# Statistics loads on another queue, and the last group's spectra packed into one block diagonal

## The chip, the cores and the metric

The kernel runs on one core of a Trainium2 chip: a tensor engine (PE), a vector engine (DVE), a scalar engine (ACT), GpSimd (POOL) and a sync engine (SP) that here only issues transfers. Transfers are also issued by ACT and GpSimd. The metric is the time of one execution on the device in microseconds, of which less is better.

## The reference

The input x holds 32 images of 32 channels of 128 x 128. Two layers are computed, each on a group-normalised x and added to it (eps 1e-5, 16 groups of two channels):

```python
# layer 1: five steps of a coupled iteration for a matrix square root, per image and channel
Y = A / norm(A); Z = I
for _ in range(5):
    T = 0.5 * (3.0 * I - Z @ Y)
    Y = Y @ T
    Z = T @ Z
x = x + Y * sqrt(norm(A))                     # A = groupnorm(x)
# layer 2: a spectral convolution
f = real(fft2(groupnorm(x)))                  # 32 low and 32 high rows, 32 columns are kept
top = einsum('bixy,ioxy->boxy', f[:, :, :32, :32], weights1)
bot = einsum('bixy,ioxy->boxy', f[:, :, -32:, :32], weights2)
x = x + real(ifft2(top and bot in their places, zeros elsewhere))
```

The second layer needs the first layer's whole image for its statistics, and its weights mix the 32 input channels at each of the 2048 kept frequencies.

## The kernel before, in words

**Iteration.** A unit of work is four channels of one image. `fetch` loads x and its transpose (tiles `b` and `xt`, 256 KB each, on ACT's queue), `staged` normalises them, and `newton` runs the iteration as a Python generator of some 13 steps: four matmuls of 128 x 128 into one PSUM bank, then an eviction by DVE (`plus`, L242) or ACT (`taken`, L234 and L236). Four lanes run such generators side by side; the main loop (L775) takes one step of each per round, so that the PE always has another lane's products to do.

**Statistics of an image.** `prep` (L160) loads the transposed image in eight tiles `xs` of 256 KB, three buffers, on SP's queue, takes `bn_stats` of each on DVE (L175), then goes through a short chain of moments, roots and reciprocals on DVE, ACT and PE, and leaves in `made` the scales that `staged` reads. One step of it is taken per round, at lane 1. Three loads are issued ahead; then each step takes the statistics of one tile and issues the load three tiles on. `stage` starts the preparation of an image when the image before it begins.

**After the iteration.** `settle` stores a finished tile to the DRAM tensor `mid` (L335, SP's queue) and folds it for the transform; `forward` and `spectrum` transform, take the second layer's statistics, and store the spectrum to the DRAM tensor `xs` of the image's group (L449). The 32 images form three groups, `GROUPS = (21, 8, 3)`.

**Products with the weights.** When a group's last spectrum is stored, `follow` starts its products. The first group goes through `wide_products`: the weights stand in a block diagonal. Groups of at most `NB = 8` images go through `small_products` (L512): the spectra stand in a block diagonal and the weights are the moving operand. A place for spectra is a tile of 128 x 2048, four diagonal blocks of 32 rows by 8 images by 64 numbers; what is off the diagonal is cleared once. There are two such tiles (`diags`) and, in the tail, three more (`late_xks`), cleared by DVE (L783). For a step `kk` of 16, 32 matmuls of 32 x 32 blocks fill a quarter of each of four column strips of PSUM; after every second step ACT copies the bank to a tile `om` (L569), which SP stores to the DRAM tensor `od` in one transfer of 256 KB (L534). SP's loads of spectra (L526) are four per pair of steps, one for each diagonal block.

**Inverse.** `inverse` loads a group's products (L590) and the tiles of `mid` (`yt`, 512 KB, L605), transforms back, adds, and stores to `out` (L613). It starts when the products of its group are all issued. Tiles `yt` alternate between six buffers and, in the tail, four more from the pool `late`. Tiles `om`, the reloaded products of a small group, and the differences `d` share three buffers tagged `page`.

**The tail.** Once no iteration is left, the pool `sets` of the iteration is closed (L779), its memory becomes the pool `late`, GpSimd loads the weights of the 14 later steps into it (L786, 512 KB each), and stores of the output go to ACT's queue.

**What sets the order.** The program is written with a tile framework which places each engine's instructions by a planner's estimate of when they are ready, and adds the waits. `kept` (`tc.keep_in_program_order`) pins an instruction behind everything written before it for its engine; nearly all transfers are pinned. Each engine, and each engine's queue of transfers, works strictly in order: a transfer that waits for its data or its buffer holds what comes after it on the issuing engine.

Of the kernel before, what the change touches and what calls it, by code (L numbers as in the profile page):

```python
# [24 lines left out]
F32 = mybir.dt.float32  # L25
# [34 lines left out]
def conv_preact_kernel(  # L60
# [32 lines left out]
    xs, od = [], []  # L93
    for i, n in enumerate(GROUPS):
        few = n <= NB
        shape = [KK // 2, P, NB, 64] if few else [KK, P, B, 32]
        xs.append(dram.tile(shape, F32, name=f"xs{i}", tag=f"xs{i}"))
        shape = [KK, 4, 4, NB, 8 * C] if few else [KK, 4, B, L * C]
        od.append(dram.tile(shape, F32, name=f"od{i}", tag=f"od{i}"))
    where = [(i, b) for i, n in enumerate(GROUPS) for b in range(n)]  # L100

# [58 lines left out]
    def prep(b, made):  # L160

        st = small.tile([P, C, 6], F32, tag="a_st", name=f"a_st{b}", bufs=2)
        tiles = []

        def load(i):
            t = stp.tile([P, 4, P], F32, tag="xs", name=f"xs{b}_{i}")
            kept(nc.sync.dma_start(out=t, in_=xt_in[b, :, 4 * i : 4 * i + 4, :]))
            tiles.append(t)

        for i in range(3):  # L170
            load(i)
        yield
        for i in range(C // 4):
            for c in range(4):
                nc.vector.bn_stats(st[:, 4 * i + c, :], tiles[i][:, c, :])  # L175
            if i + 3 < C // 4:
                load(i + 3)
            yield
        _, nm, d = yield from moments(st, "a")
        q = small.tile([P, C], F32, tag="a_qs", name=f"a_qs{b}")  # L180
        nc.vector.tensor_reduce(
            q, d.rearrange("p g (c e) -> p (g c) e", e=2), AX.X, ALU.add
        )
        yield
        pq = bank()[:, 0, 0:C]
        nc.tensor.matmul(pq, avg_mean, q, start=True, stop=True)

        v = small.tile([P, C + G], F32, tag="a_v", name=f"a_v{b}")
        nc.vector.tensor_scalar_mul(v[:, 0:C], pq, -512 / (P * P))
        yield  # L190
        vg = small.tile([P, G], F32, tag="a_vg", name=f"a_vg{b}")
        nc.vector.tensor_reduce(
            vg, v[:, 0:C].rearrange("p (g c) -> p g c", c=2), AX.X, ALU.add
        )
        nc.vector.tensor_scalar(v[:, C:], vg, 0.5, EPS, ALU.mult, ALU.add)
        s = root(v, C + G, "a_r")
        inv = small.tile([P, C + G], F32, tag="a_inv", name=f"a_inv{b}")
        nc.vector.reciprocal(inv, s)
        yield

        sc = small.tile([P, C], F32, tag="a_sc", name=f"a_sc{b}", bufs=2)
        nc.vector.tensor_scalar_mul(sc, inv[:, 0:C], 1.0 / P)
        n = small.tile([P, G, 2], F32, tag="a_n", name=f"a_n{b}")
        nc.vector.tensor_tensor(  # L204
            n,
            s[:, 0:C].rearrange("p (g c) -> p g c", c=2),
            inv[:, C:, None].to_broadcast([P, G, 2]),
            ALU.mult,
        )
        nn = small.tile([P, C], F32, tag="a_nn", name=f"a_nn{b}")  # L210
        nc.vector.tensor_scalar_mul(
            nn, n.rearrange("p g c -> p (g c)"), P * (1.5 / EYE) ** 2
        )
        sn = root(nn, C, "a_t")

        scr = small.tile([P, C], F32, tag="a_scr", name=f"a_scr{b}", bufs=2)
        nc.vector.tensor_scalar_mul(scr, sc, QR * QS)
        off = small.tile([P, G, 2], F32, tag="a_off", name=f"a_off{b}", bufs=2)
        nc.vector.tensor_tensor(
            off,  # L220
            scr.rearrange("p (g c) -> p g c", c=2),
            nm[:, :, None].to_broadcast([P, G, 2]),
            ALU.mult,
        )
        made[b] = (nm, sc, sn, scr, off.rearrange("p g c -> p (g c)"))
        yield
# [285 lines left out]
    def small_products(i):  # L512

        n = GROUPS[i]
        xks = [t.rearrange("p (b m) -> p b m", b=4 * NB) for t in diags] + late_xks
        wts = [t.rearrange("p (e q t o) -> p e q t o", e=2, q=4, t=4) for t in plain] + late_wts

        def load_weights(kk):
            if kk < 2 or not late:
                kept(nc.sync.dma_start(out=wts[kk % len(wts)], in_=wk[kk]))  # L520

        def load_spectra(k2):
            for l4 in range(4):
                rows = slice(32 * l4, 32 * l4 + 32)
                kept(
                    nc.sync.dma_start(  # L526
                        out=xks[k2 % len(xks)][rows, NB * l4 : NB * l4 + n, :],
                        in_=xs[i][k2, rows, 0:n, :],
                    )
                )  # L530

        def store(k2, om):
            kept(
                nc.sync.dma_start(  # L534
                    out=od[i][2 * k2 : 2 * k2 + 2].rearrange("e q l b x -> (q l b) e x"),
                    in_=om.rearrange("p (e x) -> p e x", e=2),
                )
            )

        if i == small_groups[0]:  # L540
            for t in diags:
                nc.gpsimd.memset(t, 0.0)
        for kk in range(2):
            load_weights(kk)
        for k2 in range(len(xks)):
            load_spectra(k2)
        done = None
        for kk in range(KK):
            yield
            k2, e = divmod(kk, 2)  # L550
            wt, xk = wts[kk % len(wts)], xks[k2 % len(xks)]
            if not e:
                pm = bank()
            for t in range(8):
                for q in range(4):
                    nc.tensor.matmul(  # L556
                        pm[32 * q : 32 * q + 32, 2 * e + t // 4, 32 * (t % 4) : 32 * (t % 4) + 32],
                        xk[:, :, 32 * e + 8 * q + t],
                        wt[:, t // 4, q, t % 4, :],
                        start=True,  # L560
                        stop=True,
                    )
            if kk + len(wts) < KK:
                load_weights(kk + len(wts))
            if done and not e:
                store(*done)
            if e:
                om = page(f"om{i}_{k2}")[:, 0:512]
                nc.scalar.copy(om, pm.rearrange("p a x -> p (a x)"))  # L569
                done = k2, om  # L570
                if k2 + len(xks) < KK // 2:
                    load_spectra(k2 + len(xks))
        store(*done)
        yield

# [3 lines left out]
    def load_products(b):  # L579
        if b < B and b not in obs:  # L580
            g, n = where[b]
            few = GROUPS[g] <= NB

            ob = page(f"or{b}") if few else inv.tile([P, 1024], F32, tag="ob", name=f"ob{b}", bufs=2)
            if few:
                src, dst = od[g][:, :, :, n, :].rearrange("k q l x -> (k q) l x"), "p (l x) -> p l x"
            else:
                src, dst = od[g][:, :, n, :].rearrange("k q x -> (k q) x"), "p (l x) -> p (l x)"
            for e in range(2):
                kept(nc.sync.dma_start(out=ob[64 * e : 64 * e + 64].rearrange(dst, l=4), in_=src))  # L590
            obs[b] = ob

    def load_input(b, e):

        if b >= B or (b, e) in yts:
            return
        yts[b, e] = []
        for i in range(2):
            o = 16 * e + 8 * i
            turn = len(yts) + i  # L600
            if late and turn % 2:
                y = late[0].tile([P, 8, P], F32, tag="yt_late", name=f"yt{b}_{o}", bufs=4)
            else:
                y = inv.tile([P, 8, P], F32, tag="yt", name=f"yt{b}_{o}", bufs=6)
            kept(nc.sync.dma_start(out=y, in_=mid[b][:, o : o + 8, :]))  # L605
            yts[b, e].append(y)
# [106 lines left out]


    late = []
    late_xks, late_wts = [], []
    small_groups = [i for i, n in enumerate(GROUPS) if n <= NB]
    lanes = [None] * LANES
    todo = [(b, g) for b in range(B) for g in range(C // 4)]
    fetches = list(todo)  # L720
# [54 lines left out]
    while todo or any(lanes) or posts or specs or prods or backs:  # L775
        tail = not todo and not any(lanes)
        if tail and not posts and not late:

            phase.close()  # L779
            late.append(ctx.enter_context(tc.tile_pool(name="late", bufs=1)))  # L780
            for i in range(3):
                late_xks.append(late[0].tile([P, 4 * NB, 64], F32, name=f"xk{i}_late"))
                nc.vector.memset(late_xks[-1], 0.0)  # L783
            for kk in range(2, KK):
                late_wts.append(late[0].tile([P, 2, 4, 4, C], F32, name=f"wt{kk}_late"))
                nc.gpsimd.dma_start(out=late_wts[-1], in_=wk[kk])  # L786
# [87 lines left out]
```

## Time and profile before

| | |
|---|---|
| time, median of three runs | 3241.55 us (3238.5 to 3243.46) |
| span of the profiled run | 3243.4 us, mean granted PE clock 0.978 |
| PE busy | 3076.9 us, 95% |
| DVE busy | 2302.2 us, 71% |
| GpSimd busy | 1761.7 us, 54% |
| ACT busy | 1462.2 us, 45% |
| transfers | 479.37 MB, mean 148 GB/s |
| statistics loads, issue to landing | 256 of 256 KB, median 3.8 us |
| loads of b, of xt, issue to landing | 256 each of 256 KB, median 2.9 and 3.2 us |

A share over the whole span hides that the program has phases. The row of PE in the page's forty slices stands at 9 (90% or more) from the second slice to the last but two, with one 8 and a few weaker stretches between; DMA traffic is about 100 GB/s in the first 24 slices and 200 GB/s after them, when the inverse transforms of the first group have begun; and the last two slices, with PE at 5 and 4, hold the tail. A wait on an engine costs time only if the PE, or in the tail the chain of transfers, comes to wait for it. So the phases are read one by one.

### The profile page before, as it was taken

To read this page: it belongs to the slowest core of one execution; us is meant where nothing else is said; L and a number is where in the kernel's file an instruction comes from. 1 tells how busy PE (TensorE), PEld (TensorE's weight loads), DVE (VectorE), ACT (ScalarE), POOL (GpSimd) and SP (SyncE) were. 2 spreads that over 40 slices of the span, in tenths; PEclk is the share of its full clock that TensorE was granted. 3 is DMA by queue.
4 is the path that set the end of the run, shared out by engine and by line. 5 is a ranking of instruction groups with operands and counts; after the bars stand their busy time and mean duration, and the time that the engine had idled before them with its cause. 6 is when DMAs were issued, how large, how long until landed. Compare 5 with 4: busy or idle time off the path is not lost.

```text
span 3243.4 us, 78214 instructions
## 1 busy us (share of the span) xinstructions
PE 3076.9 (95%) x30656; PEld 2945.4 (91%) x30656; DVE 2302.2 (71%) x6395; ACT 1462.2 (45%) x3068; POOL 1761.7 (54%) x2310
## 2 busy tenths in 40 slices
PE   6999999999999999999999999999999998999954
PEld 6999999999999999999999999998989888999853
DVE  6777777777777777777777776577777777766654
ACT  3444444444444444444444444444444444445532
POOL 4554555455455544455455454366667776746642
PEclk9999999999999999999999999999999999999985
DMA  3233333332233333333322236665666766576677
GB/s 124 97 103 102 99 105 99 101 98 94 83 100 105 102 99 105 99 102 98 101 93 90 95 100 203 212 214 198 223 224 202 248 231 223 191 221 210 200 253 266
DMA packets 271746, 479.37 MB, mean 148 GB/s; under 512 B 80656, under 2 KB 91408, under 8 KB 271376
## 3 DMA queue, kind: packets, MB, share of 16 engines
q1 hardware_dynamic: 192752, 322.28, 30.6%
q10 hardware_dynamic: 76608, 144.74, 13.9%
q0 software_dynamic: 2016, 7.34, 0.6%
q8 instruction: 242, 3.96, 0.5%
q14 instruction: 128, 1.05, 0.1%
HBM read 319.06 MB, written 155.19 MB: 146 GB/s over the span
## 4 chain that ended last, share of the span: by engine, by line
PE 79%; DMA 8%; DVE 8%; issue 2%; ACT 2%; SPq 1%; POOL 0%; DVEq 0%; ACTq 0%; POOLq 0%
PE ps L248 61%; PE ps L254 10%; DMA xs<-in_xt 6%; DVE xt L326 1%; PE ps L671 1%; PE ps L358 1%; DVE a_st L175 1%; DVE yt L688 1%; PE ps L395 1%; PE ps L556 1%; PE ps L492 1%; DMA or<-od 1%; DVE v L242 1%; PE ps L649 1%; ACT spec L437 1%
## 5 line engine op out<-in xcount | busy, mean ns | idle before, releaser
L340 POOL TENSOR_TENSOR fold<-xt 128x256 f32<-128x256 f32 x512 | 362.6, 729 | 627.2 <-DVE xt L326 566.3
L291 POOL TENSOR_TENSOR r<-b,eye 128x512 f32<-128x512 f32 x256 | 327.1, 1278 | 625.0 <-issue 604.2
L248 PE MATMUL ps<-w,v 128*128 128x128 f32 x4096 | 549.1, 277 | 2.9 <-DVE w L242 2.9
L248 PE MATMUL ps<-y,q 128*128 128x128 f32 x4096 | 545.7, 276 | 0.9 <-ACT y L234 0.9
L248 PEld LDWEIGHTS ps<-w,v 128*128 128x128 f32 x4096 | 501.5, 193 | 5.5 <-DVE w L242 4.0
L248 PEld LDWEIGHTS ps<-y,q 128*128 128x128 f32 x4096 | 501.5, 193 | 2.1 <-ACT y L234 1.3
L234 ACT COPY y<-ps 128x512 f32<-128x512 f32 x512 | 299.5, 585 | 355.9 <-PE ps L248 355.4
L272 POOL TENSOR_SCALAR x<-xt,a_nm,a_sc 128x128 f32<-128x128 f32 x1024 | 448.1, 451 | 20.8 <-DVE a_n L204 19.1
L282 ACT ACTIVATE b<-b,a_off,a_scr 128x128 f32<-128x128 f32 x1024 | 422.7, 486 | 2.1 <-DMA b<-in_x 1.8
L242 DVE SCALAR_TENSOR_TENSOR w<-ps,r 128x512 f32<-128x512 f32 x512 | 348.5, 683 | 60.0 <-PE ps L254 57.9
L242 DVE SCALAR_TENSOR_TENSOR q<-ps,eye 128x512 f32<-128x512 f32 x512 | 348.4, 682 | 59.0 <-PE ps L248 50.9
L624 POOL TENSOR_TENSOR yt<-yt,d 128x512 f32<-128x512 f32 x236 | 300.2, 1298 | 165.0 <-ACT d L683 142.8
L242 DVE SCALAR_TENSOR_TENSOR v<-ps,m 128x512 f32<-128x512 f32 x256 | 175.6, 686 | 256.9 <-PE ps L248 255.1
L315 POOL TENSOR_TENSOR r<-mb,eye 128x512 f32<-128x512 f32 x256 | 326.1, 1274 | 25.3 <-ACT mb L236 25.0
L254 PE MATMUL ps<-ident,v 128*128 128x128 f32 x2048 | 313.2, 276 | 17.1 <-DVE v L242 16.9
L236 ACT ACTIVATE mb<-ps 128x512 f32<-128x512 f32 x256 | 153.1, 598 | 387.2 <-PE ps L254 376.8
L175 DVE BATCH_NORM_STATS2 a_st<-xs 128x6 f32<-128x128 f32 x1024 | 224.0, 279 | 144.9 <-DMA xs<-in_xt 144.0
L326 DVE SCALAR_TENSOR_TENSOR xt<-ps,a_t_s,xt 128x128 f32<-128x128 f32 x1024 | 289.4, 341 | 49.7 <-PE ps L248 49.2
L248 PE MATMUL ps<-m,q 128*128 128x128 f32 x2048 | 284.6, 282 | 22.8 <-DVE q L242 21.3
L242 DVE SCALAR_TENSOR_TENSOR v<-ps,x 128x512 f32<-128x512 f32 x256 | 175.6, 686 | 181.0 <-PE ps L248 180.6
L248 PE MATMUL ps<-y,t 128*128 128x128 f32 x2048 | 281.2, 281 | 9.0 <-DVE t L242 5.4
L248 PEld LDWEIGHTS ps<-m,q 128*128 128x128 f32 x2048 | 251.2, 193 | 36.3 <-DVE q L242 22.6
(119 smaller groups left out, 5252.6 us busy)
## 6 DMA issues: line engine op xcount, KB each, us to landing
b<-in_x ACTq DMA_DIRECT2D x256, 256.0 KB, 2.9
xt<-in_xt ACTq DMA_DIRECT2D x256, 256.0 KB, 3.2
xs<-in_xt SPq DMA_DIRECT2D x256, 256.0 KB, 3.8
mid<-xt SPq DMA_DIRECT2D x256, 256.0 KB, 2.0
yt<-mid SPq DMA_DIRECT2D x128, 512.0 KB, 6.6
out<-yt SPq DMA_DIRECT2D x108, 512.0 KB, 4.6
ob<-od SPq DMA_DIRECT2D x42, 256.0 KB, 4.2
out<-yt ACTq DMA_DIRECT2D x20, 512.0 KB, 5.0
```

Source lines behind the costliest of these rows:

```text
L175: nc.vector.bn_stats(st[:, 4 * i + c, :], tiles[i][:, c, :])
L234: nc.scalar.copy(t, ps)
L242: nc.vector.scalar_tensor_tensor(s, ps, f, t, ALU.mult, ALU.add)
L248: nc.tensor.matmul(ps[:, j, :], lhsT[:, j, :], rhs[:, j, :], start=True, stop=True)
L254: nc.tensor.transpose(ps[:, j, :], t[:, j, :], ident)
L272: nc.gpsimd.tensor_scalar(m[:, j, :], xt[:, j, :], nm[:, c // 2 : c // 2 + 1], sc[:, c : c + 1], ALU.add, ALU.mult,)
L282: nc.scalar.activation(mb[:, j, :], mb[:, j, :], AF.Identity, bias=off[:, c : c + 1], scale=scr[:, c : c + 1],)
L291: nc.gpsimd.tensor_tensor(r, mb, eye, ALU.add)
L315: nc.gpsimd.tensor_tensor(r, mb, eye, ALU.add)
L326: nc.vector.scalar_tensor_tensor(xt[:, j, :], ps[:, j, :], sn[:, c : c + 1], xt[:, j, :], ALU.mult, ALU.add)
L340: nc.gpsimd.tensor_tensor(f[:, :, 64 * half : 64 * half + 64], xt[:, :, 0:64], xt[:, :, 64:128], op)
L624: engine.tensor_tensor(yh, yh, d, op)
```

## The change

It has four parts.

1. The loads of `prep` go to ACT's queue, and the load three tiles on is issued one step later: after the `yield`, ahead of the next tile's statistics. This takes them out of the queue in which stores wait for finished tiles, and lets the statistics that free a buffer end before ACT comes to the load.
2. In `small_products` a group of n < 8 images uses a block diagonal of n images, not of eight. A group of three then needs 768 columns for a place and not 2048, so that two places fit into each of the two `diags` tiles, and the three late tiles and their clearing on DVE go. The two tiles are cleared again by GpSimd for each group, since the blocks lie elsewhere. The matmuls have 4 n stationary columns; their results are 4 n rows in each quarter of the partitions, which are evicted quarter by quarter, by ACT and DVE in turn, and stored in four transfers.
3. The DRAM tensors `xs` and `od` of such a group are laid out to match: `xs` without unused images, `od` with the image innermost among 32 rows of a quarter, so that the 4 n rows of a quarter are adjacent. For the group of eight nothing changes in the layout, the places or the copies.
4. The memory gained goes to the late `yt` tiles: eight buffers and not four.

```diff
@@ prep
-            kept(nc.sync.dma_start(out=t, in_=xt_in[b, :, 4 * i : 4 * i + 4, :]))
+            kept(nc.scalar.dma_start(out=t, in_=xt_in[b, :, 4 * i : 4 * i + 4, :]))
...
                 nc.vector.bn_stats(st[:, 4 * i + c, :], tiles[i][:, c, :])
+            yield
             if i + 3 < C // 4:
                 load(i + 3)
-            yield
@@ small_products
-        xks = [t.rearrange("p (b m) -> p b m", b=4 * NB) for t in diags] + late_xks
+        parts = [slice(32 * q, 32 * q + 4 * n) for q in range(4)] if n < NB else [slice(0, P)]
+        size = 4 * n * 64
+        xks = [
+            t[:, size * j : size * j + size].rearrange("p (b m) -> p b m", m=64)
+            for t in diags
+            for j in range(2048 // size)
+        ]
...
-                        out=xks[k2 % len(xks)][rows, NB * l4 : NB * l4 + n, :],
+                        out=xks[k2 % len(xks)][rows, n * l4 : n * l4 + n, :],
...
-            kept(
-                nc.sync.dma_start(
-                    out=od[i][2 * k2 : 2 * k2 + 2].rearrange("e q l b x -> (q l b) e x"),
-                    in_=om.rearrange("p (e x) -> p e x", e=2),
+            for rows in parts:
+                kept(
+                    nc.sync.dma_start(
+                        out=od[i][2 * k2 : 2 * k2 + 2].rearrange("e q b x -> (q b) e x")[rows],
+                        in_=om.rearrange("p (e x) -> p e x", e=2)[rows],
+                    )
                 )
...
-        if i == small_groups[0]:
-            for t in diags:
-                nc.gpsimd.memset(t, 0.0)
+        for t in diags:
+            nc.gpsimd.memset(t, 0.0)
...
-                        pm[32 * q : 32 * q + 32, 2 * e + t // 4, 32 * (t % 4) : 32 * (t % 4) + 32],
+                        pm[32 * q : 32 * q + 4 * n, 2 * e + t // 4, 32 * (t % 4) : 32 * (t % 4) + 32],
...
-                nc.scalar.copy(om, pm.rearrange("p a x -> p (a x)"))
+                for j, rows in enumerate(parts):
+                    copy = nc.vector.tensor_copy if j % 2 else nc.scalar.copy
+                    copy(om[rows], pm.rearrange("p a x -> p (a x)")[rows])
@@ load_products, load_input
-                src, dst = od[g][:, :, :, n, :].rearrange("k q l x -> (k q) l x"), "p (l x) -> p l x"
+                src, dst = od[g][:, :, n : 4 * GROUPS[g] : GROUPS[g], :].rearrange("k q l x -> (k q) l x"), "p (l x) -> p l x"
...
-                y = late[0].tile([P, 8, P], F32, tag="yt_late", name=f"yt{b}_{o}", bufs=4)
+                y = late[0].tile([P, 8, P], F32, tag="yt_late", name=f"yt{b}_{o}", bufs=8)
@@ main loop, where the iteration has ended
-            for i in range(3):
-                late_xks.append(late[0].tile([P, 4 * NB, 64], F32, name=f"xk{i}_late"))
-                nc.vector.memset(late_xks[-1], 0.0)
```

More of the change, by code (lines that the diff above doesn't have):

```diff
@@ L95, in conv_preact_kernel @@
         few = n <= NB
-        shape = [KK // 2, P, NB, 64] if few else [KK, P, B, 32]
+        shape = [KK // 2, P, n, 64] if few else [KK, P, B, 32]
         xs.append(dram.tile(shape, F32, name=f"xs{i}", tag=f"xs{i}"))
-        shape = [KK, 4, 4, NB, 8 * C] if few else [KK, 4, B, L * C]
+        shape = [KK, 4, 32, 8 * C] if few else [KK, 4, B, L * C]
         od.append(dram.tile(shape, F32, name=f"od{i}", tag=f"od{i}"))
@@ L532, in store @@
         def store(k2, om):
-            kept(
-                nc.sync.dma_start(
-                    out=od[i][2 * k2 : 2 * k2 + 2].rearrange("e q l b x -> (q l b) e x"),
-                    in_=om.rearrange("p (e x) -> p e x", e=2),
-                )
-            )
-        if i == small_groups[0]:
-            for t in diags:
-                nc.gpsimd.memset(t, 0.0)
+            for rows in parts:
[4 more added lines that the diff above has]
+                    )
+                )
+        for t in diags:
+            nc.gpsimd.memset(t, 0.0)
         for kk in range(2):
@@ L715, in conv_preact_kernel @@
     late = []
-    late_xks, late_wts = [], []
-    small_groups = [i for i, n in enumerate(GROUPS) if n <= NB]
+    late_wts = []
     lanes = [None] * LANES
```

## The prediction, made before the changed kernel was run

> **What bounds the kernel now.** I read the page's busy shares first (TensorE 95% busy), then the same shares in stretches of 100 us, then the waits of the stretches that are not full, then the timeline around the longest of them. The stretches (columns: length; busy us and count of TensorE, its weight loads, VectorE, ScalarE, GpSimd; granted TensorE clock; DMA share; GB/s):
>
> ```profile
> core 0: us, PE busy (x) PEld busy (x) DVE busy (x) ACT busy (x) POOL busy (x), PEclk, DMA share, GB/s
> 300.00:400.00 100.00, 99.87 (x899) 96.87 (x898) 72.74 (x213) 45.41 (x94) 51.32 (x73) 1.00 0.30 96
> ...
> 2200.00:2300.00 100.00, 92.86 (x893) 88.70 (x892) 74.27 (x187) 46.18 (x105) 67.50 (x79) 0.97 0.56 190
> ...
> 2600.00:2700.00 100.00, 89.97 (x864) 84.01 (x862) 76.25 (x196) 44.51 (x100) 69.61 (x79) 0.97 0.70 235
> ...
> 3100.00:3200.00 100.00, 46.80 (x1348) 41.57 (x1347) 39.35 (x82) 22.93 (x50) 35.67 (x37) 0.69 0.70 243
> ```
>
> Three phases. From 100 to 2000 us TensorE is idle for 9.7 us in all: nothing taken off another engine can show there. From 2100 to 2900, where the first group's inverse transforms run beside the iteration and DMA traffic doubles, it is idle for 42.2 us (100 less each stretch's busy time, summed), and five of the eight stretches show a granted clock of 0.95 to 0.98, together 15 us of lost clock. From 3124 on no iteration is left, and the last group's products and inverses stand alone.
>
> What ends the idle time in 2100 to 2900, and what the DMA queue of SyncE waits for over the run (total us, times, longest):
>
> ```profile
> DVE a_st L175 <- DMA xs<-in_xt: 50.7, 24, 7.1
> ...
> SPq L335 <- DVE xt L326: 1410.9, 197, 24.5
> ```
>
> VectorE waits 24 times for a statistics load (xs). That load shares SyncE's queue with the stores of finished tiles (L335), which wait for the end of an iteration. The longest case in the timeline (start, length, engine, and in brackets the idle time before):
>
> ```profile
> 2625.49 1.57 SPq L605 DMA_DIRECT2D yt<-mid  x2
> 2627.10 8.17 SPq L167 DMA_DIRECT2D xs<-in_xt  x4
> 2634.04 0.87 DVE L175 BATCH_NORM_STATS2 a_st<-xs 128x6 f32<-128x128 f32 x4 [7.14 <-DMA xs<-in_xt]
> 2634.83 0.67 DVE L242 SCALAR_TENSOR_TENSOR v<-ps,x 128x512 f32<-128x512 f32 x1
> 2635.56 1.11 PE L254 MATMUL ps<-ident,v 128*128 128x128 f32 x4 [5.38 <-DVE v L242]
> ```
>
> The first loads of an image go out only at 2627.10, right behind two 512 KB loads; VectorE had come to its statistics before that and stands for 7.14 us. The v behind them on VectorE is late, and TensorE starves for 5.38 us. I set all TensorE pauses over 0.7 us between 2100 and 2900 beside the xs waits: nine end within 4 us after one (4.25, 1.89, 0.93, 0.87, 2.94, 3.24, 5.38, 1.36, 3.42), 24.3 us in all. The five long ones (4.25, 2.94, 3.24, 5.38, 3.42) lie in exactly the five stretches with the lower clock. So I put 24.3 + 15 = 39 us down to late statistics loads.
>
> The tail:
>
> ```profile
> 3130.13 1.76 DVE L783 MEMSET xk_late<- 128x2048 f32 x1 [0.38 <-issue]
> 3131.82 0.10 DVE L149 COPY b_nm<-ps 128x16 f32<-128x16 f32 x1
> 3132.30 1.76 DVE L783 MEMSET xk_late<- 128x2048 f32 x1 [0.38 <-issue]
> ...
> 3140.95 0.37 SPq L449 DMA_DIRECT2D xs<-spec  x1
> ...
> 3153.12 3.57 SPq L526 DMA_DIRECT2D diag<-xs  x8
> 3156.42 2.09 PE L556 MATMUL ps<-plain,diag 128*32 128x32 f32 x128 [17.38 <-DMA diag<-xs]
> ...
> 3195.17 1.18 SPq L590 DMA_DIRECT2D or<-od  x2
> ...
> 3210.22 15.24 SPq L605 DMA_DIRECT2D yt<-mid  x6
> ```
>
> Clearing the late spectra tiles sits on VectorE between the steps of the last image's moments. The chain goes on through the store of its spectrum, the reload, the products (3156 to 3192), the store and reload of products, and the last three inverses, whose loads of mid stand 15 us waiting for buffers.
>
> **What the Trainium skill says.** "DMA: Bandwidth & Descriptors", section Queues, rings and completion order: the queues of SyncE and ScalarE are one row of rings each, a DMA engine takes descriptors in ring order and goes round robin between rows. So a load in ScalarE's row is not behind the 512 KB loads in SyncE's. The trace agrees: in 2100 to 2900 the median landing is 3.7 us for b (ScalarE's queue) and 5.2 us for transfers that touch xs (59 of 91 are these loads), while in 100 to 2000 it is 2.9 and 3.3. The section Issuing engines are not separate DMA queues says that another issuing engine only saves issue time; the example above shows that here it also changes what a load waits behind. "TensorE: Matmul & The Clock Gate", section What's actually happening: after an idle window of about 3.4 us the clock drops to half, and comes back after about as long at work. That fits the five stretches; 15 us over five pauses is 3 us each.
>
> **The change, part by part.** *Loads to ScalarE's queue.* 256 issues leave SyncE (410 ns median each) for ScalarE, which issues b and xt in 334 and 445 ns. In 100 to 2000 that is 8 per image of some 93 us: 3 us on an engine that is busy 45%, and TensorE has ScalarE's results queued; nothing. In 2100 to 2900, 59 loads. What is queued behind such a load on ScalarE are the copies of y, m, t that TensorE waits for, so a waiting issue would hurt. The load waits for the statistics that free its buffer; putting it one step later (after the yield) lets those finish first, at the price of a lead of two steps and not three: an image takes some 105 us here for 26 rounds, 4 us a step, so 8 us against a landing of 3.7 us median, 8.6 at most. The first three loads still have one step, 4 us. At 2624 to 2626 ScalarE was not behind (d, t, y follow each other), so in the example the load would have gone out about 2.5 us sooner and landed 3.7 later, near 2628.5, leaving a wait of under 2 us, not 7. Between nothing (the one-step lead is too short) and all 39 us, I take half: -19.5. Against it stands ScalarE's standing at issues: four waits there ended by DMA (3.2, 2.3, 2.2, 2.1, together 9.8 us) for 116 issues; 59 more give 5 us, half of it felt: +2.5 (bounds 0 and, if each of 59 held ScalarE for 0.4 us and all of it showed, 24).
>
> *Start.* Image 0's loads now come behind b and xt in one ring (up to +1.5), while image 1's loads, placed behind ScalarE's first activations, no longer bring statistics between the steps of image 0's moments from 18 to 26 us (up to -3). I take -1.
>
> *Clears.* Three memsets of 1.76 us leave VectorE; the chain that ended last holds 0.88 + 1.76 + 1.76 = 4.4 us of them: -4.4. The clear of the two diagonal tiles for the last group comes to GpSimd, 2 x 1.80 us; GpSimd is idle from 3144.5 to 3167.9 and the spectrum lands at 3153 (or 3149): hidden by that transfer, 0. That transfer takes 12.2 us beside the late weights, however early it goes out, so the 4.4 us carry on.
>
> *Small products of the last group.* The same 1024 matmuls with 12 columns and not 32 stationary: TensorE's pace there (2.2 us for 128, then pauses of 1.2 to 4.6 us without a cause in the profile) stays. Four places in place of five: in the old order the last spectra load was issued at 3176.6 and needed at 3188; 16 loads, then 4 loads and 4 stores by turns at 0.42 us put the last at about 25 us after the first, product seven at 35: hidden. Stores: 32 and not 8, 24 x 0.42 = 10 us more issue on SyncE, spread over 36 us in which it waited for evictions; only the last round shows: 3 more issues (1.2) and a second half-microsecond copy per engine (0.6), less a shorter transfer (98 KB and not 256): +1.5. VectorE's copies have nothing behind them.
>
> *Eight late buffers.* The six loads at 3210 need not wait 15 us. But from 3200 to 3236 the DMA engines are 0.91 to 1.04 busy: 12 loads and 12 stores of 0.524 MB, 12.6 MB at about 0.33 MB/us, are 38 us however they are ordered. What is left are gaps: -2 (0 to -5).
>
> The group of eight keeps its layouts, places and copies: 0. Sum: -19.5 + 2.5 - 1 - 4.4 + 1.5 - 2 = -22.9, from 3241.5: 3218.6, rounded 3218.
>
> **Rivals.** (1) *The transfer is late anyway*: one step of lead is too short on ScalarE's ring too, the waits stay, only start and tail gain: 3241.5 - 1 - 4.9 = 3236. For it: the first tiles of an image have the longest waits. Against: in the example the issue itself was late. (2) *ScalarE becomes the place of the wait*: in-order behind loads that wait for VectorE's statistics or an earlier transfer, the copies that feed TensorE come late. 24 us in 2100 to 2900 and 0.2% of the first 2000 (4 us), no gain but the tail's: 3241.5 + 28 - 6 = 3263; half of it, 3250, is as likely. For it: one ScalarE wait of 3.2 us was ended by a transfer. Against: b and xt, 512 issues, cost it so little. (3) *All late loads cured*, SyncE's queue moving freely too: -39 + 2.5 - 5.9: 3199.
>
> **How the numbers follow.** Forecast 0.58, (1) 0.17, (2) 0.16, (3) 0.09. Range 3197 to 3246: from (3) through (1) and the edge of (2). Over 0.2% faster means under 3235: the forecast, (3) and a third of (1), 0.72. Within: 0.12. Slower (over 3248): 0.16.
>
> **What would show it.** Right: waits for xs in 2100 to 2900 at 25 us or less, granted clock at 0.99 or more in most of those stretches, TensorE idle there near 25 us; no memset on VectorE after 3100 and some 4 us less to the last spectrum; the last six loads issued without a pause but the end no more than a few us nearer. Wrong: ScalarE idle before y, m, t by a transfer for over 10 us, or TensorE below 99% in 100 to 2000, speak for (2); xs waits as long as before for (1). A new order of instructions along the whole program, since every one of them is placed anew, could also move some us either way in the middle phase, which none of these steps holds.

## The result, and the profile after

The kernel after takes 3229.99 us (median of 4 runs, 3225.19 to 3232.89) against 3241.64 before: ratio 0.9964 [0.9946, 0.9981], 11.7 us less. The forecast was 3218, so the sign and the range hold, and the size is half of what was forecast. The profiled executions differ by 15.5 us (3243.4 and 3227.9). They can be cut at marks that every kernel has: the issue of the stores of spectra (the transfer xs<-spec, one per image: the 1st, 21st, 31st and 32nd) and the first product of the last group. Each stretch was measured in one profiled execution per kernel. Kernels with the same code up to the end of a stretch agree there within about 3 us; in the last stretch, kernels with the same tail differ by up to 5 us.

| stretch, us | before | after | difference | forecast |
|---|---|---|---|---|
| start to 1st spectrum | 176.9 | 174.6 | -2.3 | -1 |
| 1st to 21st (nothing beside the iteration) | 1779.9 | 1764.0 | -15.9 | 0 |
| 21st to 31st (first group's inverses beside it) | 1119.3 | 1124.7 | +5.4 | -17 |
| 31st to 32nd | 64.8 | 60.6 | -4.2 | -4.4 |
| 32nd to first product | 15.5 | 18.4 | +2.9 | 0 |
| first product to the end | 87.0 | 85.6 | -1.4 | -0.5 |

The gain is not where it was forecast. Where 17 us were to come, the kernel became slower; where nothing was to come, it gained 16 us. These two errors partly cancel, so that sign and range hold by luck. Three stretches of 100 us in the kernel after (columns as before):

```profile
core 0: us, PE busy (x) PEld busy (x) DVE busy (x) ACT busy (x) POOL busy (x), PEclk, DMA share, GB/s
300.00:400.00 100.00, 99.96 (x907) 97.55 (x906) 75.51 (x221) 45.67 (x95) 51.79 (x74) 1.00 0.30 96
2200.00:2300.00 100.00, 94.64 (x918) 89.64 (x917) 75.71 (x198) 47.46 (x105) 67.60 (x80) 0.99 0.63 209
2600.00:2700.00 100.00, 90.71 (x874) 85.16 (x873) 73.79 (x188) 45.20 (x102) 70.38 (x79) 0.97 0.71 232
```

In the first line the busy share hardly moves (99.87 to 99.96), but the count of matmuls goes from 899 to 907: 0.9% more work in the same 100 us. Over 1600 us of this phase, first before, then after:

```profile
300.00:1900.00 1600.00, 1592.34 (x14350) 1542.78 (x14349) 1173.84 (x3435) 731.41 (x1512) 815.51 (x1152) 1.00 0.31 99
```

```profile
300.00:1900.00 1600.00, 1599.28 (x14478) 1555.87 (x14477) 1190.98 (x3469) 737.21 (x1525) 824.28 (x1162) 1.00 0.31 99
```

TensorE's busy time grows by 6.9 us, its matmuls by 128, which at 1600 us for 14478 are 14.1 us of work. So about half of what TensorE lost before stood in the profile as idle time; the other half lay inside what it calls busy. The busy time of its weight loads grows by 13.1 us, and the stretch from the 1st to the 21st spectrum gets 0.9% shorter, as the count says.

In this phase VectorE waited 68.8 us in 44 waits for statistics loads before, and 0.6 us in one wait after. The longest of these waits comes once in each image. In the kernel before:

```profile
354.97 0.37 SPq L449 DMA_DIRECT2D xs<-spec  x1
...
356.01 0.32 SPq L335 DMA_DIRECT2D mid<-xt  x1
...
356.38 1.98 SPq L167 DMA_DIRECT2D xs<-in_xt  x3
...
360.76 0.29 DVE L175 BATCH_NORM_STATS2 a_st<-xs 128x6 f32<-128x128 f32 x1 [2.81 <-DMA xs<-in_xt]
```

SyncE's queue stands 10.0 us before the store of a spectrum (354.97), until its data is there, and 0.6 us before the store of a tile (356.01). An image's first three statistics loads go out right behind them, and VectorE stands 2.81 us before the first. All 18 images from 300 to 1900 us show this order, with waits of 2.3 to 4.3 us.

What ends VectorE's waits for statistics in 2100 to 2900, and SyncE's largest wait over the whole run:

```profile
DVE a_st L175 <- DMA xs<-in_xt: 39.5, 14, 5.6
```

```profile
SPq L335 <- DVE xt L326: 1658.8, 198, 15.1
```

Before, these were 50.7 us in 24 waits and 1410.9. The loads no longer stand behind the finished tiles in SyncE's queue, which waits longer now and holds none of them. But in this phase 14 waits remain of 24, and they are longer in the mean (2.8 us for 2.1). TensorE is idle for 41.5 us of these 800 us (42.2 before), and seven of the eight stretches show a granted clock below 1.00, together 19 us of lost clock (15 before). One of the waits that are left:

```profile
2864.55 0.65 ACTq L262 DMA_DIRECT2D xt<-in_xt  x1
...
2865.30 1.16 ACTq L167 DMA_DIRECT2D xs<-in_xt  x1
...
2872.87 0.49 DVE L175 BATCH_NORM_STATS2 a_st<-xs 128x6 f32<-128x128 f32 x2 [5.62 <-DMA xs<-in_xt]
...
2875.03 1.38 PE L248 MATMUL ps<-m,q 128*128 128x128 f32 x8 [4.13 <-DVE q L242]
```

The load goes out at 2865.30, right behind b (2864.18) and xt, together 512 KB, of ScalarE's own row, and lands 7.6 us later. "DMA: Bandwidth & Descriptors" in the Trainium skill, section Queues, rings and completion order, says that a DMA engine takes one row's descriptors in ring order; this trace agrees: b lands at 2867.88, xt at 2869.12, xs at 2872.85. So the move put the load behind ScalarE's own loads. That is half of the 7.6 us only: a load of 512 KB that SyncE issued at 2866.00 lands at 2872.68, and how much of the second half is due to such traffic was not separated.

A cost that was small before, with one wait of 3.23 us at 2632:

```profile
2612.58 0.33 ACTq L262 DMA_DIRECT2D xt<-in_xt  x1
...
2615.01 5.86 ACTq L167 DMA_DIRECT2D xs<-in_xt  x3
...
2620.91 0.59 ACT L234 COPY m<-ps 128x512 f32<-128x512 f32 x1 [8.32 <-DMA xt<-in_xt]
2621.55 1.11 PE L254 MATMUL ps<-ident,m 128*128 128x128 f32 x4 [4.57 <-ACT m L234]
```

ScalarE stands 8.32 us at its issues, with the m that TensorE needs queued behind them. Every kernel below that kept these loads on ScalarE there shows such a hold of 8.1 to 9.5 us near this point. The trace shows what ends it. In this program the transfers of SyncE and ScalarE use eight semaphores in common, which tell of their landing, and an issue goes out only when the transfer before it on its semaphore has landed. The three loads of xs go out at 2615.01, 2619.04 and 2620.53, each 0.02 us after the landing of a transfer that SyncE had issued from 2608.84 to 2611.01 (one yt, two ob). So a late transfer of one engine holds an issue of the other. Seven of ScalarE's 172 issues in 2100 to 2900 stood in this way, for 11.1 us in all; none did from 300 to 1900. No run gave the loads semaphores of their own.

The tail:

```profile
3123.91 0.37 SPq L449 DMA_DIRECT2D xs<-spec  x1
...
3138.51 10.08 SPq L533 DMA_DIRECT2D diag<-xs  x20
...
3142.27 1.91 PE L563 MATMUL ps<-plain,diag 128*12 128x32 f32 x128 [20.27 <-DMA diag<-xs]
...
3144.23 0.57 ACT L578 COPY om<-ps 12x512 f32<-12x512 f32 x1 [20.59 <-PE ps L563]
3144.84 0.68 DVE L578 COPY om<-ps 12x512 f32<-12x512 f32 x1 [20.96 <-ACT om L578]
3145.55 0.58 ACT L578 COPY om<-ps 12x512 f32<-12x512 f32 x1 [0.75 <-DVE om L578]
3146.16 0.70 DVE L578 COPY om<-ps 12x512 f32<-12x512 f32 x1 [0.64 <-ACT om L578]
...
3195.68 11.84 SPq L614 DMA_DIRECT2D yt<-mid  x6
```

The memsets are gone, as forecast. But from the store of the spectrum to its reload now pass 14.6 us (3123.91 to 3138.51), not 12.2. The four copies of a page wait for each other by turns (2.6 us from 3144.23 to 3146.86), so splitting them over two engines wins nothing. And the six loads of mid still take 11.84 us to issue (15.24 before), though there are buffers: the third stands 7.5 us, waits for nothing but its semaphore, and goes out (3204.94) 0.02 us after the store of `out` by ScalarE that had it before.

### The profile page after: what moved, and what is told of

It is laid out like the page before. It is cut to its first block, busy times and chain, and to the rows that moved or that the text cites. A ratio compares the mean times of both kernels' runs of the same rounds, so it can differ in the third digit from the quotient of the medians.

```text
span 3227.9 us, 78350 instructions
## 1 busy us (share of the span) xinstructions
PE 3072.5 (95%) x30656; PEld 2949.3 (91%) x30656; DVE 2316.4 (72%) x6408; ACT 1467.4 (45%) x3076; POOL 1767.5 (55%) x2312
## 4 chain that ended last, share of the span: by engine, by line
PE 85%; DMA 6%; DVE 6%; ACT 1%; issue 1%; POOL 0%; SPq 0%; ACTq 0%; DVEq 0%; POOLq 0%
PE ps L248 67%; PE ps L254 11%; DMA xs<-in_xt 3%; PE ps L358 2%; PE ps L680 2%; DVE yt L697 2%; DMA or<-od 1%; PE ps L492 1%; PE ps L395 1%; PE ps L658 1%; DVE xt L326 1%; DVE a_st L175 1%; PE ps L563 1%; DMA od<-om 0%; DVE q L242 0%
## 5 line engine op out<-in xcount | busy, mean ns | idle before, releaser
L248 PE MATMUL ps<-m,q 128*128 128x128 f32 x2048 | 285.5, 283 | 18.7 <-DVE q L242 16.1
L248 PE MATMUL ps<-x,b 128*128 128x128 f32 x2048 | 273.4, 277 | 3.9 <-POOL x L272 3.9
```

The costliest lines, as they stand in the source:

```text
L248: nc.tensor.matmul(ps[:, j, :], lhsT[:, j, :], rhs[:, j, :], start=True, stop=True)
```

## The experiments

All of them compute the reference in full. The columns of the table are the stretches of above; the last two are timed. The kernel before, timed beside each of them on the same chip, had medians from 3241.64 to 3248.06 us, so compare rows by the ratio.

| kernel | start to 1st | 1 to 21 | 21 to 31 | 31 to 32 | to product | to end | ratio [95%] | median us |
|---|---|---|---|---|---|---|---|---|
| before | 176.9 | 1779.9 | 1119.3 | 64.8 | 15.5 | 87.0 | | 3241.64 |
| after | 174.6 | 1764.0 | 1124.7 | 60.6 | 18.4 | 85.6 | 0.9964 [0.9946, 0.9981] | 3229.99 |
| loads_only | 174.2 | 1764.1 | 1125.8 | 65.3 | 14.9 | 88.1 | 0.9959 [0.9947, 0.9972] | 3230.76 |
| tail_only | 176.0 | 1777.2 | 1119.8 | 60.6 | 18.7 | 86.9 | 1.0003 [0.9994, 1.0012] | 3243.49 |
| queue_only | 178.5 | 1764.2 | 1111.9 | 60.6 | 18.4 | 89.5 | 0.9946 [0.9932, 0.9959] | 3225.53 |
| step_only | 176.8 | 1782.1 | 1118.9 | 60.6 | 18.6 | 89.1 | 1.0002 [0.9993, 1.0011] | 3245.84 |
| queue_lead | 174.5 | 1765.0 | 1116.6 | 60.0 | 17.8 | 88.1 | 0.9945 [0.9929, 0.9961] | 3225.78 |
| step_lead | 173.9 | 1765.0 | 1118.8 | 60.1 | 18.3 | 89.3 | 0.9947 [0.9932, 0.9962] | 3226.55 |
| queue_hybrid | 177.8 | 1764.8 | 1123.8 | 60.7 | 18.8 | 88.2 | 0.9966 [0.9954, 0.9979] | 3235.85 |
| weights_later | 174.5 | 1764.2 | 1122.8 | 62.4 | 7.1 | 102.1 | 0.9967 [0.9954, 0.9980] | 3233.46 |
| queue_pinned | 176.5 | 1783.6 | 1090.5 | 60.2 | 18.6 | 89.5 | 0.9918 [0.9904, 0.9931] | 3219.94 |
| queue_lead_pinned | 175.2 | 1784.6 | 1093.2 | 60.6 | 17.4 | 90.2 | 0.9932 [0.9919, 0.9944] | 3222.97 |
| step_lead_pinned | 173.9 | 1784.3 | 1098.1 | 63.4 | 18.0 | 88.7 | 0.9931 [0.9918, 0.9945] | 3224.28 |
| pinned_from_22 | 177.7 | 1765.5 | 1083.5 | 60.5 | 17.1 | 89.8 | 0.9872 [0.9855, 0.9888] | 3199.08 |

### Which part, and the queue or the step

loads_only is the kernel before with the two edits to the statistics' loads; tail_only is the kernel after without them. queue_only and step_only split those two edits in the kernel after:

```
queue_only                              step_only
     bn_stats of tile i                      t loaded with nc.sync.dma_start
+    if i + 3 < C // 4: load(i + 3)          (not nc.scalar)
     yield                                   bn_stats of tile i
-    if i + 3 < C // 4: load(i + 3)          yield; load(i + 3)
```

> The kernel before with the first part of the change alone: statistics loads on ACT's queue, one step later; group of three and late buffers as before. Theory A (the loads bring about 2 us at the start and 16 us up to the 21st spectrum, and then lose about 6 us again while the inverses run; the packing of the last group brings about 4 us): ratio 0.9970 to 0.9980, 21st spectrum stored near 1939 us, the chain of the last spectrum 4 us longer than in the changed kernel. Theory B (the order of instructions fell better by chance, and the tail's edits did that as much as the loads): 21st spectrum anywhere between 1939 and 1957 us.

> The changed kernel with the statistics loads put back on SP's queue and ahead of the yield, so that only the packing of the last group and the eight late buffers are left. Theory A: 21st spectrum near 1957 us as in the kernel before, ratio 0.9985 to 0.9995 (2 to 5 us from the tail). Theory B: the 21st spectrum moves, too.

> The changed kernel with the load issued before the yield again, in the step of the statistics that free its buffer, but on ACT's queue. My reasoning (ACT would stand at the issue until VectorE has done the statistics, with the copies for TensorE behind it): slower than the changed kernel by 3 to 15 us, with more idle time of ACT ended by a_st. The rival (the place of the yield does not matter, the planner puts the load where it is ready): the same as the changed kernel within 2 us.

> The changed kernel with the statistics loads on SP's queue, but issued after the yield. If the queue makes the gain of the first 2000 us (Theory A): 21st spectrum near 1957 us or later, ratio 0.999 to 1.003. If the later issue makes it (rival): 21st spectrum near 1939 us, ratio 0.996 to 0.998.

The eight kernels with these loads on ScalarE's queue and the statistics unpinned at least until image 22 need 1764.0 to 1765.5 us from the 1st to the 21st spectrum; the three with SyncE's need 1777.2 to 1782.1. So the queue makes the early gain, and neither the tail's edits nor the later issue do. The new placement of every instruction, which differs between these kernels, moves it by 1.5 and 5 us at most. VectorE's waits for xs up to 1900 us go with it: 89.1 us before, 84.1 in tail_only, 137.3 in step_only; 10.2 after, 10.0 in loads_only, 12.7 in queue_only. The sum of these waits is not their price, though. Against tail_only, step_only has 53 us more of them and takes 5 us longer; queue_only has 71 us less and takes 13 us less: 0.1 to 0.2 us for each us of wait.

In the middle phase queue_only was the surprise: it takes 1111.9 us there against 1124.7 for after and 1125.8 for loads_only. I had expected the earlier issue to make the kernel slower. For the whole time only that it isn't slower is safe, as the intervals overlap (0.9946 [0.9932, 0.9959] and 0.9964 [0.9946, 0.9981]). The wait at 2872.87 shown above is not in its trace. But these 13 us are not the price of the later issue in general. In the other pairs of kernels that differ in it alone, the later issue costs 2.2 us (step_lead against queue_lead) and 4.9 us (step_lead_pinned against queue_lead_pinned, below), and on SyncE's queue it gains 0.9 (step_only against tail_only). The new placement of the instructions can have a share in the 13 us that no run separates. In the start the order is reversed: 178.5 against 174.6.

The tail's edits together bring nothing that can be measured (1.0003 [0.9994, 1.0012]), against 4.9 us forecast.

### More lead by one more step

> Loads on ACT's queue and ahead of the yield (as in queue_only), and one more step between an image's first three loads and its first statistics. Theory C (while the inverses run, an image's first tiles are waited for because one step, 4 us, is shorter than a landing of 5 to 8 us in the crowded queues): waits of VectorE for statistics loads from 2080 to 3060 us fall from 42 to under 25 us, and ten images from the 21st to the 31st spectrum take 4 to 8 us less than the 1112 us of queue_only. Rival D (those waits are not what stops TensorE there): the waits fall, the ten images take the same 1112 us within 3.

> The changed kernel with one more step between an image's first three loads and its first statistics; the later loads still go out one step later than in queue_only. Theory C: from the 21st to the 31st spectrum 1118 us or less, where the changed kernel takes 1124.7. If it is the lead of two steps for tiles three to seven that costs the time there: still 1122 or more.

Both add one `yield` after the first three loads of an image. With the later issue the lead gains 6 us (after 1124.7, step_lead 1118.8); with the earlier it loses 5 (queue_only 1111.9, queue_lead 1116.6). So it has no effect of one sign, and both forecasts are missed, step_lead's by 0.8 us. Neither cures the waits (43.0 and 37.2 us from 2080 to 3060, after 42.5). The timeline of queue_lead shows why:

```profile
2491.50 1.09 ACTq L263 DMA_DIRECT2D xt<-in_xt  x1
...
2494.05 0.33 ACTq L167 DMA_DIRECT2D xs<-in_xt  x1
...
2499.71 0.49 DVE L176 BATCH_NORM_STATS2 a_st<-xs 128x6 f32<-128x128 f32 x2 [3.17 <-DMA xs<-in_xt]
```

Two steps, of some 4 us each, are written between the load and its statistics, and still VectorE comes to them 2.5 us after the load's issue and stands there for 3.17 us. The statistics are not pinned, so the planner is free to put them on VectorE as early as it takes the data to be there. A step in the text is not a lead on the chip.

### The statistics pinned

> As queue_only, with the statistics pinned in VectorE's order and no more steps of lead. If it is the pin that helps: as queue_lead_pinned. If the lead is needed beside it (Theory C): waits for statistics loads between 25 and 45 us, and the ten images at 1108 to 1114 us.

> As queue_lead (loads on ACT's queue ahead of the yield, one more step before an image's first statistics), with the statistics pinned in VectorE's order as written. In queue_lead the waits stayed, 43 us, and the first load of the 26th image still went out only 5.7 us before VectorE stood at its statistics: the planner had pulled them forward. Theory C, kept alive by that: pinned, the waits of VectorE for statistics loads from 2080 to 3060 us fall under 15 us, and 1100 to 1108 us from the 21st to the 31st spectrum; ratio 0.990 to 0.9935. Rival D (the waits do not set the time there): the waits fall and the ten images stay at 1112 to 1117.

> The changed kernel (later loads one step later) with one more step before an image's first statistics and the statistics pinned. Theory C: the first tiles' waits go, those of tiles three to seven, with two steps of lead of about 4 us each in the order as written, mostly too; waits under 20 us, the ten images 1104 to 1114 us, the early stretch 1764 us as in every kernel with the loads on ACT's queue.

Each wraps one line in queue_only, queue_lead and step_lead, so that VectorE meets the statistics at their written place:

```
-  nc.vector.bn_stats(st[:, 4 * i + c, :], tiles[i][:, c, :])
+  kept(nc.vector.bn_stats(st[:, 4 * i + c, :], tiles[i][:, c, :]))
```

The waits from 2080 to 3060 fall to 6.0, about 0 and 1.6 us, and the middle phase to 1090.5, 1093.2 and 1098.1: 21 us below the best unpinned kernel, 29 below before. The pin does it alone: queue_pinned has no step of lead, and it is the fastest of the three. But the early phase loses its gain (1783.6 to 1784.6), where 1764 had been expected of step_lead_pinned. In queue_pinned's timeline of the early phase:

```profile
1002.00 0.86 DVE L175 BATCH_NORM_STATS2 a_st<-xs 128x6 f32<-128x128 f32 x4
1002.78 1.27 DVE L242 SCALAR_TENSOR_TENSOR q<-ps,eye 128x512 f32<-128x512 f32 x2
1003.51 1.16 PE L248 MATMUL ps<-m,q 128*128 128x128 f32 x8 [0.36 <-DVE q L242]
```

At a pinned place the statistics run ahead of the q that TensorE needs next; TensorE waits 0.36 us. From 300 to 1900 us there are 19 such waits, about one in an image of 88 us, 6.8 us in all; queue_only has none. As in the kernel before, this is less than what was lost: TensorE does 158 matmuls less than in queue_only (14319 and 14477), some 17 us of work or 1 us per image. The rest lies inside its busy time, and how it comes about is not shown.

### Pinned only where they wait

> As queue_pinned, with the statistics pinned in VectorE's order for images 22 to 31 alone (counted from 0), those whose statistics are taken beside the inverses. If the two stretches answer to two things (before the inverses the waits were all that was lost, and a pinned order costs a microsecond per image; beside the inverses the planner's pulling forward makes the waits): 1764 us from the 1st to the 21st spectrum as with the loads on ACT's queue and free statistics, 1090 to 1097 from the 21st to the 31st as in the pinned kernels, together 20 us less than queue_pinned: near 3200 us, ratio 0.985 to 0.988. If the gain of the pinned kernels there depends on the order further ahead: over 3212 us.

```
+  pin = kept if b >= 22 else lambda ins: ins
-  nc.vector.bn_stats(st[:, 4 * i + c, :], tiles[i][:, c, :])
+  pin(nc.vector.bn_stats(st[:, 4 * i + c, :], tiles[i][:, c, :]))
```

On queue_only. It keeps both gains: 1765.5 early, 1083.5 in the middle, 3199.08 us in all, the fastest of the series. Stretch 2100 to 2900 of after, then of pinned_from_22, and the latter's waits for xs from 2080 to 3060:

```profile
2100.00:2900.00 800.00, 758.49 (x7865) 719.13 (x7863) 595.49 (x1561) 370.98 (x823) 534.90 (x632) 0.98 0.66 216
```

```profile
2100.00:2900.00 800.00, 777.39 (x8413) 737.20 (x8414) 608.81 (x1608) 387.09 (x854) 551.26 (x652) 1.00 0.68 224
```

```profile
DVE a_st L176 <- DMA xs<-in_xt: 7.1, 3, 5.6
```

548 more matmuls in the same 800 us (7%; 4.4% without the last 100 us, where the kernel that is ahead already does more of the second group's small products), and the clock back at 1.00. What is left is one stretch: 2600 to 2700, busy 90.19, where ScalarE again stands 8.4 us at an issue.

TensorE's pauses and its clock account for the whole middle phase. In all fourteen kernels the stretch from the 21st to the 31st spectrum is 1048 to 1052 us, plus TensorE's idle time there, plus what a lower clock took (half of the time in which the clock was at half). The sum is 1050.0 + 50.5 + 18.8 us before, 1049.5 + 34.2 + 6.8 in queue_pinned, and 1050.8 + 31.0 + 1.7 in pinned_from_22. The last two have the same code from image 22 on and differ by 7 us; why is not shown.

### Is ScalarE's queue a burden beside the inverses?

> As queue_only, but images 22 to 31 load their statistics on SP's queue again, so that only the stretch before the inverses has them on ACT's. If ACT's queue helps in both stretches: 21st spectrum near 1943 us as in queue_only, and 1118 to 1121 us from the 21st to the 31st spectrum as with SP's queue. If standing at the issues on ACT costs more than it brings beside the inverses: 1108 or less.

```
+  kept((nc.scalar if b < 22 else nc.sync).dma_start(out=t, ...))   # on queue_only
```

Not with the earlier issue: with SyncE's queue for the last ten images the middle phase takes 1123.8 us against 1111.9 for queue_only, although the hold of 8 us on ScalarE is part of the latter. With the later issue it is the other way round: 1118.9 on SyncE's queue (step_only), 1124.7 on ScalarE's (after). So without the pin the runs do not settle which queue is better beside the inverses.

### What the last spectrum's store waits for

> The changed kernel with ten of the fourteen late weight loads moved from GpSimd, where they go out as the iteration ends, to SP's queue behind the first spectra loads of the last group. Theory E (the last spectrum's store lands when the 7.3 MB of late weights have drained, so that what comes before its issue cannot show): landing falls from 14.6 us to 4 to 7, first product 7 to 10 us sooner after the store's issue than the 18.4 us of the changed kernel; the end gains less, -4 to +3 us, since the weights are then waited for. Rival (the store is slow by its 256-byte pieces): landing stays over 11 us.

GpSimd loads four of the fourteen late weights, and SyncE the other ten behind the last group's spectra:

```
   for kk in range(2, KK):
+      if kk < 6: nc.gpsimd.dma_start(out=late_wts[-1], in_=wk[kk])
   # in small_products, after the first spectra loads
+  if late: for kk in range(6, KK): kept(nc.sync.dma_start(out=late_wts[kk - 2], in_=wk[kk]))
```

```profile
3123.87 0.37 SPq L449 DMA_DIRECT2D xs<-spec  x1
...
3126.73 8.48 SPq L533 DMA_DIRECT2D diag<-xs  x16
...
3130.92 1.86 PE L566 MATMUL ps<-plain,diag 128*12 128x32 f32 x123 [8.96 <-DMA diag<-xs]
```

The same store now lands in 2.9 us (3123.87 to 3126.73), and the first product comes 7.1 us after it, not 18.4. The weights have to come all the same: the last stretch grows to 102.1, and from the 31st spectrum to the end it takes 7 us more than after, where -4 to +3 were expected. So the store's 12 to 15 us were the late weights' traffic. The landings say the same: the last of the fourteen weights lands at 3152.89 before and 3139.18 after, the store at 3153.11 and 3138.49; in weights_later the four weights have landed (3122.99) before the store goes out.

## Where the prediction failed and where it held

The forecast of the gain failed in three terms: 0 for the early phase (-15.9 measured), -17 for the middle phase (+5.4), and 0 for the way from the last spectrum's store to the first product (+2.9).

**Early phase: wrong.** The step that failed is "TensorE is idle for 9.7 us in all: nothing taken off another engine can show there". It took a busy share of 99.5% for full work. SyncE's queue was the cause that it had named, but for the middle phase alone. The same trace held the sign to the contrary: VectorE's waits for xs were there too (89.1 us up to 1900), and a matmul's end in the profile is modelled. The count of matmuls shows 0.9% to be had, and queue_only against tail_only shows that the queue gives it. How a wait of VectorE of 1.5 us in the mean (89.1 in 61) slows TensorE inside its busy time is not shown.

**Middle phase: the cause right, the cure wrong.** The 39 us put down to late loads were a fair bound: with these waits nearly gone the stretch falls by 29 us (queue_pinned) and 36 (pinned_from_22) against before. They were a little high: the clock of before was at half six times in 2100 to 2900, for 3.41 or 6.83 us, and one of these times (2728) follows no wait for statistics. The change left 39.5 us of VectorE's waits, where 25 or less were to show the forecast right. What failed is "8 us against a landing of 3.7 us median, 8.6 at most", and so the half taken of it. First, a written step is no lead while the planner may pull statistics forward (queue_lead against queue_lead_pinned). Second, a load behind b and xt in its own ring can take longer than the median (7.6 us at 2865.30). Third, the later issue, which the prediction counted as a protection of ScalarE, did not pay on ScalarE's queue: it cost 2 to 13 us in three pairs of kernels. The term for ScalarE's standing, +2.5, was too small as well. It rested on four waits of 9.8 us ended by transfers in the kernel before, where the view of its waits has one, of 3.2 us. After, there are four, 15.7 us in all, and the hold at 2612 alone stopped TensorE for 4.57 us. The prediction looked at loads that wait for VectorE; this one waited for SyncE's transfers, through the semaphores. One pause of after has another origin: at 2543.75 a subtraction of 128x64 on VectorE took 4.95 us (0.24 in the median of 32, 1.69 the next longest) beside GpSimd operations, and TensorE paused 4.64 us behind it. That the two engines hinder each other is only argued.

Rival (1), "the waits stay, only start and tail gain", describes the middle phase better than the forecast did, but its 3236 left out the early gain. Rival (2) came in small: ScalarE stood at issues, but the early phase, where it forecast a loss of 4 us, gained 16.

**Tail: the clears right, their gain lost.** 4.2 us less between the last two spectra answer to the forecast 4.4. The step that failed is "That transfer takes 12.2 us beside the late weights, however early it goes out, so the 4.4 us carry on". GpSimd's loads of the 7.3 MB of late weights start at 3124.5 before and at 3111.6 after, and the spectrum's reload follows 28.6 and 26.9 us later, whenever its store went out (16.4 and 12.3 us after that start). The store ends when the weights do, within 0.7 us. weights_later shows it by taking them away. In the last stretch -0.5 was forecast and -1.4 seen in after, with 86.9 to 90.2 in other kernels with the same tail: not resolved. There the price of the split copies was too low: four in a row, 2.6 us, not two beside two. "PSUM — Partial Sum Buffer" in the Trainium skill, section PSUM bank collisions raise a hardware error, says that different quadrants of one bank may be accessed at once; here each copy waits for the one before, so no run shows it. The forecast of -2 for the late buffers rested on loads that need not wait; one of them waited for a semaphore instead.

**Start: right** in sign (-2.3 for -1). With the earlier issue on ScalarE's queue it is +1.6 (queue_only), and with one more step before the first statistics -2.4 (queue_lead). So the gain needs more than the queue.

## What to carry to other kernels

When a bottleneck engine is 99% busy, count its instructions per stretch before calling it full: here 899 against 907 matmuls in 100 us, behind a busy share that moved by 0.1, are 16 us in the phase. To bring data earlier, look at what stands before the load in its queue and at what may pull its reader forward: a step written between them did not keep the reader back, pinning the reader did, with or without that step. Pinning it where nothing waited cost more than the queue had won (19 us for 16). When an issue stands though its data and its buffer are ready, look at what else it waits for: here it was a semaphore that a transfer of another engine still held. A few us taken off a chain are lost when its next link is a transfer that ends with somebody else's traffic.

## What the runs showed of the hardware

A store of one image's spectrum (256 KB) landed in 2.9 us when no late weights were under way, and in 12.2 and 14.6 us beside them, within 0.7 us of the last weight (weights_later, before, after). In 2100 to 2900 of the kernel before, five pauses of TensorE of 2.9 to 5.4 us each went with 3.41 or 6.83 us at half the clock; a sixth such time came with pauses of 0.6 and 0.8 us.

"DMA: Bandwidth & Descriptors" in the Trainium skill, section Issuing engines are not separate DMA queues, has the choice of issuing engine as a matter of issue time; here 256 loads moved from SyncE to ScalarE are worth 16 us in the early phase alone, and not by issue time: on SyncE they stood behind stores that waited 10 us for their data.
